# A fused involution block: another order for the norm chain, another engine for the constant part

## The chip, the cores and the metric

The kernel runs on one core of a Trainium2 chip. Its engines are PE (TensorE, matmuls; PEld is its weight load), DVE (VectorE), ACT (ScalarE), POOL (GpSimd) and SP (SyncE, which here only issues DMAs). Each engine takes its own instructions in order and waits on semaphores for the others. The metric is the device time of one execution in microseconds (us).

## The reference, cut to what matters

The input is x of 8 images, 256 channels, 56 x 56, in float32. Two layers follow each other:

```
x = x + involution(group_norm(x))            # this is where the change is
x = x + tri_conv_block(group_norm(x))        # two 3x3 convolutions, batch norms, ReLU
```

The involution makes, for each pixel, a 7 x 7 kernel for each of 16 groups of channels, and applies it to the pixel's neighbourhood:

```
ker = w_reduce @ v + b_reduce                # 64 channels, v = group_norm(x)
ker = w_span @ ker + b_span                  # 16 groups x 49 taps
out = (ker * patches(v)).sum(taps)           # zero padding of 3
```

Group norm is v = rstd * x + shift, with one rstd and one shift (-mean * rstd) per image and group. As it is linear, the sum over taps splits in two: rstd times the sum over the raw x, and shift times the sum of the kernel's 49 taps. The second is called the constant part here. It is itself a small matmul of the reduced `ker` with the taps' summed weights, plus the summed bias.

## The kernel before, in words

The involution is the first stage, to about 1031 us; two convolutions and a last elementwise stage follow, which the change does not touch.

The involution works by quarters: `quarters` (L1034) lists 8 images x 4 quarters c of 64 channels, and in a quarter both halves of the image's height lie side by side on 128 partitions. Each quarter has 10 rows `ty` of three image lines. r = c * 10 + ty numbers the rows of an image from 0 to 39. A row has, in the order of the text (L1055 to L1086):

- `apply_row` (PE, L905): the row's matmuls of neighbourhoods `q` with the kernels `a` into a PSUM tile `pa`, of which there are two. `prefetch` issues the load of a later `q` on SP's queue, and stores and loads of x are issued ahead of it.
- a step of the generator `norm`, if one is running.
- `gn2_stats` and `gn1_stats` (DVE, L153): bn_stats for the next layer's norm and for the next image's. The latter is spread over r = 4 to 19, one piece a row.
- `pick_out`: ACT scales the first part of `pa` into `inv` (L915), DVE adds the rest (L917), POOL adds `inv` to x (L922).
- `surround`: POOL adds the rim to a later `q` (L797); ACT fills its end (L810). `rim_of` prepares the rim in row 1.
- a second step of `norm`.
- `PER_ROW[ty]` steps of `gen`, the generator of the next quarter's kernels (`generate`).
- in rows 24 to 34 of an image, a strip of `reduce` for the next image (PE L759, ACT L768 into `kr`, with the bias `brn`).
- a step of `quant`, which quantizes the convolutions' weights on DVE (L314 to L334, tiles `piece_w`).

`pin` then fixes this order on every engine; no scheduler changes it.

`generate` has 14 units. A unit takes a pair of the six PSUM banks of `ps_p`, fills them by PE (L867, `pg`), and has one bank emptied by ACT with a bias (L871) and the other by DVE (L881). A pair is used again three units later, by a unit, by a strip or by the constant part. Units 0 to 5 read kr[0], units 6 to 9 kr[1], units 10 to 13 kr[2].

After its units, `generate` runs `constant` in two steps. Each has PE make the sums in a pair of banks (L832, `ks`), ACT turn them into `add` with the scale and the bias of the norm (L840), and POOL add `add` to x (L847); in the very last quarter DVE does that addition. Image lines of phase 0, 1, 2 have 504 columns each; the fourth piece is the last line of a half, with 56. In the steady loop both steps fall in row 8.

`params`, the norm chain of the next image, starts in r = 20 and is advanced twice a row, once ahead of the pick-out and once behind it. Its steps before the change:

- 20, ahead: matmul of the group means (L160), which needs the last bn_aggr.
- 20, behind: DVE's L164, L168, L169 (deviation `d`, squared).
- 21, ahead: matmul of `d` (L172).
- 21, behind: variance and `ve` (DVE L175, L139), the square root (ACT L141), the reciprocal and its Newton step (L143 to L149), scale and shift (L177, L178), and the image's scaled weights `wrn`, `scales`, `shift` (L670, L677, L680), all in one block.
- 23, ahead: matmuls of the reduce bias (L686); 23, behind: `brn` (L689).
- 24, ahead: rim matmuls (L696) and their copy by ACT (L700).

The small matmuls L160, L172 and L686 write to the spare columns of the current row's `pa`. In the last image, `gn2_params` takes the place of `params`: the same chain up to the norm's scale and shift, for the second layer. The first image's chain runs in the setup, as does the first quarter's `generate`.

Of the kernel before, what the change touches and what calls it, by code (L numbers as in the profile page):

```python
# [8 lines left out]
F32 = mybir.dt.float32  # L9
F32R = mybir.dt.float32r  # L10
AF = mybir.ActivationFunctionType
ALU = mybir.AluOpType
# [5 lines left out]
P = 128  # L18
B, C, H, W = 8, 256, 56, 56
# [5 lines left out]
GN_EPS = 1e-5  # L25
# [4 lines left out]
NCQ = C // CH  # L30
# [31 lines left out]

PER_ROW = (2, 2, 2, 1, 2, 2, 1, 2, 2, 0)
NQB = 5
# [3 lines left out]
NCB = 4  # L68
NC = NHW // NCB


# [20 lines left out]
def involution_tri_block_kernel(  # L92
# [41 lines left out]

    def rstd_of(var, eps, name):

        n = var.shape[1]
        ve = small.tile([P, n], F32, tag=f"rs_ve{n}", name=f"ve_{name}")
        nc.vector.tensor_scalar(ve, var, eps, None, ALU.add)  # L139
        sq = small.tile([P, n], F32, tag=f"rs_sq{n}", name=f"sq_{name}")  # L140
        nc.scalar.activation(sq, ve, AF.Sqrt)  # L141
        r0 = small.tile([P, n], F32, tag=f"rs_r0{n}", name=f"r0_{name}")
        nc.vector.reciprocal(r0, sq)  # L143
        e = small.tile([P, n], F32, tag=f"rs_e{n}", name=f"e_{name}")
        nc.vector.tensor_tensor(e, r0, ve, ALU.mult)
        nc.vector.tensor_tensor(e, e, r0, ALU.mult)
        nc.vector.tensor_scalar(e, e, -0.5, 1.5, ALU.mult, ALU.add)
        r = small.tile([P, n], F32, tag=f"rs_r{n}", name=f"r_{name}")
        nc.vector.tensor_tensor(r, r0, e, ALU.mult)  # L149
        return r  # L150

# [3 lines left out]
    def group_norm_params(mv, dst, psum_tile, name, means=None):  # L155
# [19 lines left out]
        nc.vector.tensor_tensor(var, ps2[:, :n], gm[:, :, 1], ALU.add)  # L175
        rs = rstd_of(var, GN_EPS, name)
        nc.vector.tensor_copy(dst[:, :, 0], rs)  # L177
        nc.vector.scalar_tensor_tensor(dst[:, :, 1], gm[:, :, 0], -1.0, rs, ALU.mult, ALU.mult)  # L178

# [440 lines left out]
    with ExitStack() as ph1:  # L620
# [6 lines left out]
        def ps_pair(name):  # L627
            return [ps_bank(f"{name}_{i}") for i in range(2)]
# [34 lines left out]
        def params(b, sums=None):  # L663
# [20 lines left out]
            for c in range(NCQ):  # L684
                for i in range(2):
                    nc.tensor.matmul(ps[i * CR:(i + 1) * CR, :1], wr[:CH, c, :], dst[:CH, c, 1:2],  # L686
                                     start=(c == 0), stop=(c == NCQ - 1))
            yield
            nc.vector.tensor_tensor(brn, br, ps[:, :1], ALU.add)  # L689
            yield  # L690
            if sums is not None:
# [127 lines left out]
        def constant(b, c):  # L819

            n = (TY - 1) * TX
            xv = xs[b, c][:, :(TY - 1) * PY * W].rearrange("p (t y w) -> p y t w", y=PY, w=W)
            scale, bias = prm[b][0][:, c, 1:2], prm[b][2][:, c:c + 1]
            for i0 in (0, 2):
                ps = ps_pair(f"ks_{b}_{c}_{i0}")
                add = work.tile([P, 2 * PX * n], F32, tag="add", name=f"add_{b}_{c}_{i0}")
                for i in range(2):
                    py = (i0 + i) % PY
                    k0, m = (0, n) if i0 + i < PY else (NT, TX)
                    rows = slice(i * CR, (i + 1) * CR)  # L830
                    for h in range(2):
                        nc.tensor.matmul(ps[i][h * CH:(h + 1) * CH, :PX * m], wsx[rows, c, :],  # L832
                                         kr[py][rows, :, k0 + h * m:k0 + (h + 1) * m],
                                         start=True, stop=True)
                for i in range(2):
                    py = i0 + i
                    m = n if py < PY else TX
                    v = add[:, i * PX * n:i * PX * n + PX * m].rearrange(
                        "p (t w) -> p t w", w=W)
                    nc.scalar.activation(  # L840
                        v.rearrange("p t (k x) -> p t k x", x=PX),
                        ps[i][:, :PX * m].rearrange("p (x t k) -> p t k x", x=PX, k=TX),
                        AF.Identity, bias=bias, scale=scale)
                    x_ = xv[:, py] if py < PY else xs[b, c][:, PY * (TY - 1) * W:].rearrange(
                        "p (t w) -> p t w", w=W)
                    engine = nc.vector if (b, c) == (B - 1, NCQ - 1) else nc.gpsimd
                    engine.tensor_tensor(x_, x_, v, ALU.add)  # L847
                yield

        def generate(b, c, a, shared=()):  # L850

            whole, rest = (v.rearrange("q t (g p) -> q g p t", g=GQ) for v in views(a))
            for u, (gp, p0, n) in enumerate(UNITS):
                ps = ps_pair(f"pg_{b}_{c}_{u}")
# [28 lines left out]
                yield  # L885
            yield from constant(b, c)

# [21 lines left out]
        def pick_out(b, c, ty, ps, n, m):  # L909
# [95 lines left out]
        first = params(0, sums)  # L1005
        for _ in range(8):
            next(first)
        nc.scalar.dma_start(wl, w_line)
# [39 lines left out]
        for m, (b, c) in enumerate(quarters):  # L1048
# [6 lines left out]
            for ty in range(TY):  # L1055
# [196 lines left out]
```

## Time and profile before

| | us |
|---|---|
| median of 3 runs (lowest, highest) | 2143.46 (2142.48, 2144.44) |
| the profiled execution | 2144.3 |
| its span, first to last instruction | 2142.5 |
| busy in the span: PE, DVE, ACT, POOL | 1750.4, 1760.6, 1428.7, 584.1 |
| first row of the loop, start | 56 |
| last row of the loop, start | 1031 |

A line of a group of instructions reads: source line, engine, operation, output<-inputs with their shape, count | busy time in us, mean ns of one | idle time of the engine just before them, and what ended it. A line of waits reads: who waited <- for whom: total us, times, longest. In a timeline the first two numbers are start and length in us, and the bracket at the end is the idle time before it and what ended that. "issue" is a time for which the profile shows nothing waited for. Line numbers are those of the kernel before.

### The profile page before, as it was taken

To read this page: it belongs to the slowest core of one execution; us is meant where nothing else is said; L and a number is where in the kernel's file an instruction comes from. 1 tells how busy PE (TensorE), PEld (TensorE's weight loads), DVE (VectorE), ACT (ScalarE), POOL (GpSimd) and SP (SyncE) were. 2 spreads that over 40 slices of the span, in tenths; PEclk is the share of its full clock that TensorE was granted. 3 is DMA by queue.
4 is the path that set the end of the run, shared out by engine and by line. 5 is a ranking of instruction groups with operands and counts; after the bars stand their busy time and mean duration, and the time that the engine had idled before them with its cause. 6 is when DMAs were issued, how large, how long until landed. Compare 5 with 4: busy or idle time off the path is not lost.

```text
span 2142.5 us, 70728 instructions
## 1 busy us (share of the span) xinstructions
PE 1750.4 (82%) x29680; PEld 1621.5 (76%) x29680; DVE 1760.6 (82%) x3360; ACT 1428.7 (67%) x3537; POOL 584.1 (27%) x960
## 2 busy tenths in 40 slices
PE   5898898989898897988799999998999999960000
PEld 5787777868777686877799999998999999950000
DVE  6778879787777878777899999998999999984444
ACT  4877787877778687777466666665676666653343
POOL 1655566555655555565000000000000000000000
PEclk9999999999999899999899999999999999985555
DMA  5767677686757768677633333335333333369999
GB/s 186 235 181 235 208 237 237 198 254 199 254 180 245 223 179 254 180 205 210 235 123 123 123 123 123 123 123 203 112 139 125 120 126 123 122 270 428 430 429 393
DMA packets 155370, 440.06 MB, mean 205 GB/s; under 512 B 63006, under 2 KB 73116, under 8 KB 147628
## 3 DMA queue, kind: packets, MB, share of 16 engines
q1 hardware_dynamic: 149760, 403.89, 55.2%
q10 hardware_dynamic: 5004, 31.56, 3.5%
q8 instruction: 235, 3.85, 0.7%
q14 instruction: 83, 0.68, 0.1%
q0 software_dynamic: 288, 0.08, 0.0%
HBM read 323.28 MB, written 112.20 MB: 203 GB/s over the span
## 4 chain that ended last, share of the span: by engine, by line
PE 69%; DVE 11%; DMA 9%; issue 5%; ACT 4%; POOL 1%; SPq 0%; ACTq 0%; POOLq 0%; DVEq 0%
PE c L561 39%; PE pg L867 15%; PE pa L905 9%; PE pk L759 4%; DMA y1f<-y1d 3%; DMA x1f<-x1d 2%; ACT a L871 2%; PE ks L832 2%; DMA out_y<-x1f 2%; DMA y2f<-y2d 1%; DVE inv L917 1%; DVE x1f L1164 1%; DVE a L881 1%; DVE st L153 1%; ACT add L840 1%
## 5 line engine op out<-in xcount | busy, mean ns | idle before, releaser
L561 PE MATMUL c<-pl,wq 128*128 128x392 f32 x4608 | 858.0, 349 | 11.3 <-ACT pl L433 9.2
L561 PEld LDWEIGHTS c<-pl,wq 128*128 128x128 f32 x4608 | 855.1, 190 | 13.9 <-ACT pl L433 9.6
L871 ACT ACTIVATE a<-pg,bt 126x126 f32<-126x126 f32 x2028 | 524.8, 457 | 110.8 <-PE pg L867 110.5
L867 PE MATMUL pg<-kr,wl 64*126 64x140 f32 (+1 forms) x6144 | 456.3, 291 | 43.2 <-ACT a L871 17.3
L867 PEld LDWEIGHTS pg<-kr,wl 64*126 64x126 f32 x6144 | 395.3, 194 | 72.7 <-issue 28.5
L905 PE MATMUL pa<-a,q 126*32 126x48 f32 x17024 | 289.0, 215 | 63.7 <-issue 55.6
L905 PEld LDWEIGHTS pa<-a,q 126*32 126x32 f32 x17024 | 241.1, 116 | 128.9 <-issue 86.8
L881 DVE TENSOR_TENSOR a<-pg,bt 126x504 f32<-126x504 f32 (+4 forms) x640 | 280.8, 481 | 37.4 <-PE pg L867 35.9
L922 POOL TENSOR_TENSOR x<-x,inv 128x168 f32<-128x168 f32 x310 | 161.1, 520 | 394.9 <-DVE inv L917 355.4
L917 DVE SCALAR_TENSOR_TENSOR inv<-pa,gn1s,inv 128x168 f32<-128x168 f32 (+1 forms) x384 | 134.0, 351 | 156.3 <-ACT inv L915 153.4
L410 ACT CAST pl<-r 128x812 fp32r<-128x812 f32 x190 | 160.7, 868 | 130.8 <-DVE r L405 121.5
L386 POOL MEMSET xp<- 128x116 f32 x32 | 6.3, 196 | 828.4 <-DVE a L405 805.1
L797 POOL TENSOR_TENSOR q<-q,sides 126x256 f32<-126x256 f32 (+1 forms) x320 | 225.7, 706 | 7.8 <-DMA q<-in_x_nb 7.8
L411 DVE TENSOR_TENSOR pl<-r,pl 128x812 fp32r<-128x812 f32 x190 | 185.3, 1002 | 28.0 <-ACT pl L410 26.7
L491 ACT ACTIVATE dummy<-y,nc 128x1568 f32<-128x1568 f32 (+1 forms) x128 | 200.2, 1564 | 4.8 <-DVE y L581 3.5
L915 ACT ACTIVATE inv<-pa,gn1s 128x168 f32<-128x168 f32 x320 | 133.3, 417 | 62.8 <-PE pa L905 47.6
L153 DVE BATCH_NORM_STATS2 st<-x 128x6 f32<-128x392 f32 x256 | 138.0, 555 | 7.9 <-DMA x<-in_x 7.4
L847 POOL TENSOR_TENSOR x<-x,add 128x504 f32<-128x504 f32 x124 | 123.2, 1024 | 12.6 <-ACT add L840 12.6
L1131 ACT ACTIVATE xp<-raw,bi_bn,sc_bn 128x392 f32<-128x392 f32 (+1 forms) x125 | 83.0, 721 | 60.3 <-DVE a L405 58.9
L1111 ACT ACTIVATE xp<-raw,gn 128x392 f32<-128x392 f32 (+1 forms) x125 | 83.3, 721 | 52.7 <-DVE a L405 51.6
L1162 DVE SCALAR_TENSOR_TENSOR y1f<-y2f,sc_bn,y1f 128x3136 f32<-128x3136 f32 (+2 forms) x20 | 56.6, 2831 | 62.8 <-DMA y2f<-y2d 52.5
L759 PE MATMUL pk<-x,wrn 64*128 64x168 f32 (+1 forms) x1152 | 101.8, 317 | 0.1
(186 smaller groups left out, 1812.0 us busy)
## 6 DMA issues: line engine op xcount, KB each, us to landing
q<-in_x_nb SPq DMA_DIRECT2D x320, 448.0 KB, 4.2
raw<-x1d SPq DMA_DIRECT2D x32, 812.0 KB, 7.0
raw<-y1d SPq DMA_DIRECT2D x32, 812.0 KB, 5.9
x1d<-x SPq DMA_DIRECT2D x64, 392.0 KB, 5.2
x<-in_x SPq DMA_DIRECT2D x60, 392.0 KB, 5.2
y1d<-y SPq DMA_DIRECT2D x30, 784.0 KB, 3.3
y2d<-y SPq DMA_DIRECT2D x30, 784.0 KB, 3.8
y1f<-y1d SPq DMA_DIRECT2D x14, 1568.0 KB, 15.1
```

The lines of the kernel that those rows point to most:

```text
L153: nc.vector.bn_stats(st[:, j, :], xt[:, j * NC:(j + 1) * NC])
L410: nc.scalar.copy(hi, r)
L411: nc.vector.tensor_tensor(lo, r, hi.bitcast(F32), ALU.subtract)
L491: nc.scalar.activation(dst, v, f, bias=shift[:, to:to + 1], accum_out=stats[:, to, j, n:n + 1])
L561: nc.tensor.matmul(ps[:, to, :NM], wq[k][:, t, dx, to * P:(to + 1) * P], part[:, t, :, dx:dx + W], start=(c == 0), stop=(c == last))
L759: nc.tensor.matmul(ps[h][:, :m * W], wrn[rows, c, :], src[rows, r0:r0 + (m - 1) * PY + 1:PY, :], start=(c == 0), stop=(c == NCQ - 1))
L797: nc.gpsimd.tensor_tensor(v, v, z, ALU.add)
L867: nc.tensor.matmul(dst, wl[rows, c, gp, o:o + NQ], kr[py][rows, px, :], start=True, stop=True)
L871: nc.scalar.activation(dst[:, g + 1, p0 + j], ps[1][:NQ, j * nt + t0:j * nt + t1], AF.Identity, bias=bt[:, c, g + 1, p0 + j:p0 + j + 1])
L881: nc.vector.tensor_tensor(dst[:, g, p0:p0 + n].rearrange("q p t -> q t p"), ps[0][:NQ, t0 * n:t1 * n].rearrange("q (t p) -> q t p", p=n), ...
L905: nc.tensor.matmul(ps[o:o + m, k * w:(k + 1) * w], q[:NQ, k, o:o + m], av[:, t + k, g * w:(g + 1) * w], start=True, stop=True)
L922: engine.tensor_tensor(xv, xv, iv.rearrange("p t (y x) -> p y t x", x=PX), ALU.add)
```

## The change

Three things are done.

The constant part leaves ACT and POOL. DVE reads the sums from PSUM, multiplies by the norm's shift and adds x in one instruction, in place. The norm's bias, which does not depend on the pixel, goes into the pick-out's activation. The pieces are paired anew: phase 0 and the last line (both from kr[0]) come in one step right after unit 5, phases 1 and 2 (kr[1], kr[2]) in the last step. With the new `PER_ROW` the steps fall in row 3 and row 8, rows 4 to 7 have two units each, and row 3 has none. In quarter 2, row 3 (r = 23) comes ahead of the strips of rows 24 to 27 that write kr[0].

The norm chain gets two steps more: the generator stops ahead of the square root and behind it. `ve` is made in 21 behind, the square root in 22 ahead, and the block from the reciprocal on in 22 behind. The reduce bias's matmuls and `brn` share a step, 24 ahead; the rim comes in 25 behind.

The statistics of the next image end in r = 18, which has two pieces, and no longer in 19.

```diff
-PER_ROW = (2, 2, 2, 1, 2, 2, 1, 2, 2, 0)
+PER_ROW = (2, 2, 2, 1, 2, 2, 2, 2, 1, 0)
+CONST_AT = 5
...
+STATS_AT = {r: (r - 4,) for r in range(4, 18)} | {18: (14, 15)}
...
-    def rstd_of(var, eps, name):
+    def rstd_of(var, eps, name, rs):
...
         sq = small.tile([P, n], F32, tag=f"rs_sq{n}", name=f"sq_{name}")
+        yield
         nc.scalar.activation(sq, ve, AF.Sqrt)
+        yield
         r0 = small.tile([P, n], F32, tag=f"rs_r0{n}", name=f"r0_{name}")
...
-        return r
+        rs.append(r)
...
-        rs = rstd_of(var, GN_EPS, name)
-        nc.vector.tensor_copy(dst[:, :, 0], rs)
-        nc.vector.scalar_tensor_tensor(dst[:, :, 1], gm[:, :, 0], -1.0, rs, ALU.mult, ALU.mult)
+        rs = []
+        yield from rstd_of(var, GN_EPS, name, rs)
+        nc.vector.tensor_copy(dst[:, :, 0], rs[0])
+        nc.vector.scalar_tensor_tensor(dst[:, :, 1], gm[:, :, 0], -1.0, rs[0], ALU.mult, ALU.mult)
...
-            yield
             nc.vector.tensor_tensor(brn, br, ps[:, :1], ALU.add)
-            yield
+            yield "bias"
+            for _ in range(2):
+                yield
...
-            scale, bias = prm[b][0][:, c, 1:2], prm[b][2][:, c:c + 1]
-            for i0 in (0, 2):
-                ps = ps_pair(f"ks_{b}_{c}_{i0}")
-                add = work.tile([P, 2 * PX * n], F32, tag="add", name=f"add_{b}_{c}_{i0}")
-                for i in range(2):
-                    py = (i0 + i) % PY
-                    k0, m = (0, n) if i0 + i < PY else (NT, TX)
+            for pair in ((0, PY), (1, 2)):
+                ps = ps_pair(f"ks_{b}_{c}_{pair[0]}")
+                for i, py in enumerate(pair):
+                    k0, m = (0, n) if py < PY else (NT, TX)
...
-                    nc.scalar.activation(
-                        v.rearrange("p t (k x) -> p t k x", x=PX),
-                        ps[i][:, :PX * m].rearrange("p (x t k) -> p t k x", x=PX, k=TX),
-                        AF.Identity, bias=bias, scale=scale)
...
-                    engine = nc.vector if (b, c) == (B - 1, NCQ - 1) else nc.gpsimd
-                    engine.tensor_tensor(x_, x_, v, ALU.add)
+                    x_ = x_.rearrange("p t (k x) -> p t k x", x=PX)
+                    nc.vector.scalar_tensor_tensor(
+                        x_, ps[i][:, :PX * m].rearrange("p (x t k) -> p t k x", x=PX, k=TX),
+                        prm[b][0][:, c, 1:2], x_, ALU.mult, ALU.add)
                 yield
...
+            made = constant(b, c)
             for u, (gp, p0, n) in enumerate(UNITS):
...
                 yield
-            yield from constant(b, c)
+                if u == CONST_AT:
+                    next(made)
+                    yield
+            yield from made
...
-            nc.scalar.activation(iv, parts[:, :, 0], AF.Copy, scale=scale[:, 0:1])
+            nc.scalar.activation(iv, parts[:, :, 0], AF.Identity, bias=prm[b][2][:, c:c + 1],
+                                 scale=scale[:, 0:1])
...
-                if more and 4 <= r < 20:
-                    gn1_stats(b + 1, (r - 4) // NCB, (r - 4) % NCB)
+                for k in STATS_AT.get(r, ()) if more else ():
+                    gn1_stats(b + 1, k // NCB, k % NCB)
```

More of the change, by code (lines that the diff above doesn't have):

```diff
@@ L832, in constant @@
                         nc.tensor.matmul(ps[i][h * CH:(h + 1) * CH, :PX * m], wsx[rows, c, :],
-                                         kr[py][rows, :, k0 + h * m:k0 + (h + 1) * m],
+                                         kr[py % PY][rows, :, k0 + h * m:k0 + (h + 1) * m],
                                          start=True, stop=True)
-                for i in range(2):
-                    py = i0 + i
+                for i, py in enumerate(pair):
                     m = n if py < PY else TX
-                    v = add[:, i * PX * n:i * PX * n + PX * m].rearrange(
-                        "p (t w) -> p t w", w=W)
-                    nc.scalar.activation(
-                        v.rearrange("p t (k x) -> p t k x", x=PX),
-                        ps[i][:, :PX * m].rearrange("p (x t k) -> p t k x", x=PX, k=TX),
-                        AF.Identity, bias=bias, scale=scale)
                     x_ = xv[:, py] if py < PY else xs[b, c][:, PY * (TY - 1) * W:].rearrange(
                         "p (t w) -> p t w", w=W)
-                    engine = nc.vector if (b, c) == (B - 1, NCQ - 1) else nc.gpsimd
-                    engine.tensor_tensor(x_, x_, v, ALU.add)
+                    x_ = x_.rearrange("p t (k x) -> p t k x", x=PX)
+                    nc.vector.scalar_tensor_tensor(
+                        x_, ps[i][:, :PX * m].rearrange("p (x t k) -> p t k x", x=PX, k=TX),
+                        prm[b][0][:, c, 1:2], x_, ALU.mult, ALU.add)
                 yield
@@ L1005, in involution_tri_block_kernel @@
         first = params(0, sums)
-        for _ in range(8):
-            next(first)
+        while next(first) != "bias":
+            pass
         nc.scalar.dma_start(wl, w_line)
```

## The prediction

> **What bounds the kernel now.** I looked first at the page's busy line and slices. No engine is the bound of the whole: PE and DVE both stand at 82% of the span, and the slices show three stages, the involution (to about 1031 us), two convolutions and a tail. Every edit is in the involution, so I read that stage alone.
>
> ```profile
> PE 1750.4 (82%) x29680; PEld 1621.5 (76%) x29680; DVE 1760.6 (82%) x3360; ACT 1428.7 (67%) x3537; POOL 584.1 (27%) x960
> ```
>
> The second view was busy time by stretch, in us, for the four quarters of one image, 0 to 3 in order, and for the stretch behind its norm chain. Columns: stretch, length, busy time of PE, PEld, DVE, ACT, POOL, then the granted PE clock and DMA.
>
> ```profile
> 669.60:698.39 28.79, 23.79 (x750) 19.56 (x748) 24.05 (x66) 22.55 (x82) 19.30 (x31) 1.00 0.88 294
> 698.39:728.21 29.82, 24.71 (x751) 20.83 (x748) 28.23 (x78) 22.12 (x80) 17.12 (x28) 0.94 0.76 234
> 728.21:768.00 39.79, 35.94 (x864) 31.25 (x862) 28.33 (x86) 27.58 (x96) 21.99 (x34) 0.87 0.54 159
> 768.00:797.10 29.10, 27.64 (x810) 23.90 (x808) 21.06 (x58) 23.90 (x88) 14.20 (x25) 1.00 0.71 201
> 738.90:749.10 10.20, 9.58 (x162) 8.29 (x162) 7.02 (x32) 5.42 (x24) 3.37 (x7) 0.50 0.45 121
> ```
>
> So the last quarter is PE's (95%). Quarter 1 is DVE's (95%). Quarter 2, with the norm chain, is 10 us longer than its neighbours, and 10.2 us of it run at half the PE clock. The third view was the waits of PE from 56 to 1031 us (total, times, longest).
>
> ```profile
> PE pa L905 <- issue: 55.6, 51, 3.9
> PE pg L867 <- ACT a L871: 17.1, 16, 2.4
> PE pg L867 <- DVE a L881: 10.8, 8, 2.2
> PE pa L905 <- POOL q L797: 4.8, 6, 1.6
> PE pa L172 <- DVE d_a L169: 4.5, 4, 1.2
> PE pa L160 <- DVE mv L661: 3.9, 3, 1.5
> ```
>
> "issue" falls in the middle of runs of like matmuls; the change has as many matmuls, so I leave it. The timeline then says what lies behind the other rows. First, the end of a quarter:
>
> ```profile
> 698.41 4.07 POOL L847 TENSOR_TENSOR x<-x,add 128x504 f32<-128x504 f32 x4
> 698.64 1.13 DVE L322 TENSOR_SCALAR piece_w<-piece_w 128x48 f32<-128x48 f32 x1
> 701.09 1.20 DVE L330 SCALAR_TENSOR_TENSOR piece_w<-piece_w 128x48 f32<-128x48 f32 x1
> 705.09 1.86 PE L867 MATMUL pg<-kr,wl 64*126 64x140 f32 x12 [1.99 <-DVE a L881]
> ```
>
> L322 and L330 take 0.19 and 0.20 us when undisturbed; under POOL's L847 they take 1.1 to 1.2. DVE falls behind, its L881 comes late, and PE waits 1.99. Second, the norm chain, rows 20 to 22:
>
> ```profile
> 732.08 1.17 DVE L169 TENSOR_TENSOR d_a<-d_a 128x4 f32<-128x4 f32 x1
> 733.30 0.39 PE L172 MATMUL pa<-d_a,grp_sb 128*128 128x4 f32 x2 [1.06 <-DVE d_a L169]
> 737.99 0.20 ACT L141 ACTIVATE sq_a<-ve_a 128x4 f32<-128x4 f32 x1 [3.80 <-DVE ve_a L139]
> 739.09 0.83 PE L867 MATMUL pg<-kr,wl 64*126 64x140 f32 x2 [2.37 <-ACT a L871]
> ```
>
> ACT stands 3.80 us at the square root with row 21's L871 behind it; those hold the PSUM banks, so PE waits 2.37, and then runs at half clock.
>
> [...] L330 is blocked, the L881 of 504 elements, one input from PSUM, stays at 0.68. [...]
>
> **Part one, the constant part (32 quarters).**
> Removed from ACT: L840, 96 of 771 ns and 32 of 405 ns, 67.2 + 13.0 = 80.2 us. Removed from POOL: L847, 115.1 + 9.4 = 124.5 us. Removed from DVE: 4 of L847 in the last quarter, 2.7 us.
> Added to DVE: 96 long and 32 short scalar_tensor_tensor from PSUM. Long ones at the 678 ns of L881's 504-element form (same source, same size): 65.1. Short ones at the 272 ns of L917's 56-element form: 8.7. Sum 73.8. [...] The strided read is not seen on DVE; if it costs as much as DVE's own blocked L847 (867 ns) the sum grows by 18.
> Given back to DVE: the piece_w operations cost some 83 us more than at their minimum (for L331, (512 - 195) ns x 64 = 20; the other eight likewise). POOL's L847 has 22% of POOL's time, so at least 18; matched by overlap about 34. I take 26. DVE net: 73.8 - 2.7 - 26 = +45 us, 1.4 a quarter.
> Added to ACT: pick-out's L915 gets a bias pointer. [...] In rows where DVE waits for L915 (120.3 us in all) [...] PE has slack there: I take 3 us lost, 0 to 9.
> What PE may get back: waits for L881, 10.8; for POOL's q, 4.8; for DVE's inv, 2.5; and half-clock stretches of 3.4 us at 182.5, 452, 705 and 834, half of 13.6 = 6.8. Together 24.9. Not all: quarters 0 and 1 have DVE at 84 to 95%, and 1.4 us more a quarter leaves part of the stall, now for DVE's own work. I take 18, from -15 (16 DVE-bound quarters x 0.9) to 25. The setup's constant part, ahead of row 0, loses 4 L840 and 4 us of POOL: +2.
> The unit moved from row 3 to row 6 makes rows 4 to 7 four full ones. [...] ACT falls back about 1.5 us; three bank pairs cover about that, and rows 8 and 9, now without L840, let it catch up. Cost nothing; if the cover is gone, 1.4 us x 31 = 43.
>
> **Part two, the norm chain (7 images and the last one's gn2 form).**
> The cost now: waits at L160 3.9, at L172 4.5 + 1.0, at L867 behind ACT 17.1, 26.5 in all. Half clock in rows 20 to 26: 51.0 us over the images, of which PE is busy 48.9; half of it is lost, 24.5. Sum 51.
> L160: the statistics end in row 18 and not 19, so this wait goes. One bn_stats (0.56) only changes rows.
> L172: it keeps its place; d and d*d lose the blocking (L169 0.27 instead of 1.17), but DVE brings 1.26 us of constant part from row 18. 0.7 a time stays: 5.6.
> Square root: `ve` is made in row 21 and read in row 22, so ACT's 3.8 goes, and 17.1 with it.
> The rest of the chain is a block on DVE, about 3.7 us in the timeline (reciprocal to gn1b), now in row 22 ahead of that row's four L881. PE finds cover in row 23 (pa 0.73, ks 0.7) and in pa and br of row 24 (0.73 + 0.8); the L881s end some 1.5 us later. So PE's next unit in row 24 waits 1.5, and the strip, whose banks the constant part's two DVE reads hold, 0.5. Another new wait: brn now stands ahead of row 24's pick-out, so ACT's L915 waits for DVE there, with row 24's L871 behind it; it ends about when DVE's L881 do. 2.0 x 7 = 14. The br matmuls and the rim only change rows. No DMA is added or moved.
> Half clock left: I take 10 of 24.5. Left in all: 5.6 + 14 + 10 = 29.6. Gain 51 - 29.6 = 21.4, from 0 to 51.
>
> **Sum.** 21.4 + 18 + 2 - 3 = 38.4. The profiled execution took 2144.3 us, span 2142.5 and 1.8 around it; 2144.3 - 38.4 = 2105.9. It lies 0.8 above the median of the runs, so 2105.
>
> **Rivals.**
> A, the forecast: both parts pay in part. 2105, own range 2090 to 2122. Chance 0.55.
> B, all relieved: both stalls go, as the PE-bound last quarter suggests, and DVE's block is hidden. 51 + 25 gives 2068; I allow 2066 to 2090. Against it: DVE at 95% in quarter 1. Chance 0.16.
> C, the wait moves: DVE's added 45 us eat the gain of part one, and the block in row 22 with the wait on brn eats most of part two. Gain 10, 2133, range 2122 to 2148. For it: DVE's shares. Chance 0.19.
> D, slower: DVE becomes the bound. If its 45 us come on the path in full and the read from PSUM takes the 867 ns (+18), part two's 21 and the setup's 2 do not pay: 2143.5 + 63 - 23 = 2183 at the worst; 2160 as a middle. [...] Chance 0.10.
>
> Measurement tells 0.2%, 4.3 us, from no change. Faster: A, B and 0.14 of C, 0.85; same 0.05; slower 0.10. The range leaves out the lower part of B and D with the end of C: 2074 to 2141.
>
> **What would show it.** PE's waits for the square root's row (L867 behind ACT) go from 17.1 to under 5, and the wait before the mv matmul is gone. piece_w operations drop by 18 to 34 us in sum. The new DVE operation takes about 0.68 us. DVE's share in quarter 1 stays above 93%. Quarter 2 goes from 38 to 35 us, quarters 0 and 1 from 29 to 28. After the chain's block a wait for DVE appears at row 24. I am wrong if quarters 0 and 1 grow, which is D, if rows 6 and 7 show PE waiting for L871, or if PE's stalls return as "issue", which would hold the gain down.

## The result

| | before | after |
|---|---|---|
| median of the runs of the comparison, us | 2144.44 | 2132.84 |
| profiled execution, us (its span) | 2144.3 (2142.5) | 2127.57 (2125.8) |
| loop, first to last row, us | 975.0 | 959.9 |

The ratio of after to before is 0.9937, with a 95% interval from 0.9923 to 0.9952. The change gains 0.63%, some 13.5 us, where 38.4 were forecast. Medians differ from chip to chip (before alone had medians from 2141 to 2153 over the comparisons below), so every experiment is read by its ratio to the runs of before on its own chip. 0.1% is 2.1 us. Where two kernels are compared through before, their ratios are divided; the interval of such a quotient is about 0.3% either side, and that the ratio of after to before is the same on each of the chips is taken for granted. Line numbers in a run's view are those of its own kernel.

Busy time of the engines of after:

```profile
PE 1737.7 (82%) x29680; PEld 1606.0 (76%) x29680; DVE 1778.4 (84%) x3484; ACT 1376.1 (65%) x3409; POOL 462.3 (22%) x836
```

ACT has lost 53 us, of the 80.2 that the forecast took from it with L840, and POOL 122, for the forecast's 124.5. DVE has gained 18 and not 45. Then the same quarters of the same image as before the change, and the stretch behind its norm chain (row 24). Columns: stretch, length, busy time of PE, PEld, DVE, ACT, POOL, granted PE clock, DMA share and GB/s.

```profile
664.49:695.81 31.32, 27.33 (x740) 22.41 (x741) 25.42 (x69) 20.59 (x76) 15.24 (x27) 0.84 0.86 265
695.81:728.28 32.47, 25.75 (x744) 21.85 (x741) 28.80 (x85) 21.54 (x77) 13.17 (x25) 0.89 0.74 227
728.28:764.52 36.24, 33.06 (x848) 28.54 (x849) 28.69 (x90) 24.30 (x88) 15.40 (x27) 0.95 0.57 167
764.52:794.10 29.58, 27.39 (x807) 23.54 (x806) 21.24 (x61) 23.70 (x86) 13.07 (x24) 1.00 0.66 197
738.81:747.36 8.55, 6.35 (x123) 5.80 (x121) 8.17 (x31) 2.86 (x10) 3.36 (x6) 0.80 0.53 161
```

In this image quarter 2 is 3.6 us shorter, but quarters 0 and 1 are each over 2.5 us longer, at a lower granted clock (0.84 for 1.00, 0.89 for 0.94). Over images 1 to 6 the mean lengths of quarters 0 to 3 went from 29.32, 29.17, 38.28 and 28.33 us to 30.75, 29.13, 35.67 and 28.14. So quarter 2 gained 2.6 an image, near the 3 that were forecast, and quarter 0 gave 1.4 of it back. The latter need not be the change's doing: in e1 below, whose quarter 0 has the instructions of before, its mean is 30.99 us, so single executions differ by as much. The waits of PE in after's loop (total, times, longest):

```profile
PE pa L908 <- issue: 66.0, 60, 4.1
PE pg L867 <- issue: 16.8, 12, 2.7
PE pa L177 <- DVE d_a L174: 6.0, 6, 1.9
PE pg L867 <- DVE a L881: 3.9, 8, 1.0
PE pk L766 <- DVE x L844: 3.3, 4, 1.1
...
PE pg L867 <- ACT a L871: 0.5, 1, 0.5
```

L867 behind ACT went from 17.1 to 0.5 and L867 behind DVE from 10.8 to 3.9. The wait ahead of the first norm matmul (L160 before, L165 now) is gone, and the one for POOL's q fell from 4.8 to 0.3. The wait at the second norm matmul (L177, L172 before) stayed: 7.8 with its smaller lines, 5.5 before. And "issue" has grown from 69.5 to 82.8 us. The timeline of after's norm chain, for the same image:

```profile
735.96 0.20 ACT L145 ACTIVATE sq_a<-ve_a 128x4 f32<-128x4 f32 x1 [0.40 <-DVE ve_a L142]
736.40 0.74 PE L867 MATMUL pg<-kr,wl 64*126 64x140 f32 x6 [0.81 <-DVE a L881]
...
740.46 0.45 PE L692 MATMUL pa<-gn,wr 64*64 64x1 f32 x9 [0.84 <-DVE gn L184]
...
742.27 0.39 PE L692 MATMUL pa<-gn,wr 64*64 64x1 f32 x7 [1.36 <-issue]
```

The square root holds ACT for 0.40 us where it held it for 3.80. What is late next is DVE's block, ahead of row 24's bias matmul. The end of quarter 0 in the timeline of after shows DVE's L328 and L336 (L322 and L330 before) undisturbed:

```profile
697.01 0.19 DVE L328 TENSOR_SCALAR piece_w<-piece_w 128x48 f32<-128x48 f32 x1
698.50 0.20 DVE L336 SCALAR_TENSOR_TENSOR piece_w<-piece_w 128x48 f32<-128x48 f32 x1
```

**An account of the loop.** I summed, from the records of PE's matmuls between the first and the last row, the idle time that ends in "issue", all other idle time, and the time at a lowered clock, of which half is taken as lost (the granted clock was 0.50 in each of these stretches of before and after). What is left over is between 799 and 816 us in every kernel of this study, most near 805, so these three terms carry most of the difference from kernel to kernel. One profile is one execution, though; the verdicts rest on the ratios.

| us in the loop | length | "issue" | other waits | lowered clock |
|---|---|---|---|---|
| before | 975.0 | 70.5 | 47.4 | 90.7 |
| after | 959.9 | 84.8 | 31.1 | 74.6 |
| e1, norm chain alone | 977.6 | 78.9 | 46.5 | 90.6 |
| e2, constant part alone | 970.5 | 89.4 | 29.3 | 93.7 |
| e7, POOL's work put back | 979.5 | 68.8 | 50.8 | 111.2 |
| e9, half of the q loads, short lead | 977.1 | 53.2 | 60.4 | 102.0 |
| e12, DVE relieved by ACT | 981.1 | 100.8 | 29.6 | 97.1 |
| e15, half of the q loads, full lead | 946.0 | 74.0 | 24.1 | 85.7 |
| e18, x loads early | 966.4 | 89.2 | 26.3 | 94.6 |

From before to after the other waits fell by 16.3 and "issue" rose by 14.3. PE is idle as long as before (117.9 and 115.9). Of the 15.1 us by which this loop of after is shorter, 8 are half of the lowered clock, 2 are idle time, and 5 are in the rest.

### The profile page after: what moved, and what is told of

The parts are those of the page before. It is cut to its first block, busy times and chain, and to the rows that moved or that the text cites. A ratio compares the mean times of both kernels' runs of the same rounds, so it can differ in the third digit from the quotient of the medians.

```text
span 2125.8 us, 70519 instructions
## 1 busy us (share of the span) xinstructions
PE 1737.7 (82%) x29680; PEld 1606.0 (76%) x29680; DVE 1778.4 (84%) x3484; ACT 1376.1 (65%) x3409; POOL 462.3 (22%) x836
## 4 chain that ended last, share of the span: by engine, by line
PE 69%; DVE 12%; DMA 10%; issue 5%; ACT 4%; POOL 0%; SPq 0%; ACTq 0%; DVEq 0%; POOLq 0%
PE c L567 40%; PE pg L867 14%; PE pa L908 8%; PE pk L766 4%; DMA x1f<-x1d 4%; DMA y1f<-y1d 2%; ACT a L871 2%; PE ks L836 2%; DVE a L881 2%; DVE inv L921 1%; DVE x1f L1168 1%; DVE x L844 1%; DMA out_y<-x1f 1%; DVE st L158 1%; DMA y2f<-y2d 1%
## 5 line engine op out<-in xcount | busy, mean ns | idle before, releaser
L871 ACT ACTIVATE a<-pg,bt 126x126 f32<-126x126 f32 x2028 | 516.6, 457 | 82.2 <-PE pg L867 79.7
L867 PE MATMUL pg<-kr,wl 64*126 64x140 f32 (+1 forms) x6144 | 441.4, 290 | 24.2 <-issue 16.8
L867 PEld LDWEIGHTS pg<-kr,wl 64*126 64x126 f32 x6144 | 391.5, 194 | 46.0 <-issue 19.9
L908 PEld LDWEIGHTS pa<-a,q 126*32 126x32 f32 x17024 | 236.5, 114 | 158.4 <-issue 100.4
L918 ACT ACTIVATE inv<-pa,gn1b,gn1s 128x168 f32<-128x168 f32 x320 | 162.5, 508 | 160.8 <-PE pa L908 104.4
L766 PEld LDWEIGHTS pk<-x,wrn 64*128 64x128 f32 x1152 | 91.8, 192 | 16.8 <-issue 9.6
## 6 DMA issues: line engine op xcount, KB each, us to landing
y1f<-y1d SPq DMA_DIRECT2D x14, 1568.0 KB, 15.1
```

The source lines that it names most:

```text
L766: nc.tensor.matmul(ps[h][:, :m * W], wrn[rows, c, :], src[rows, r0:r0 + (m - 1) * PY + 1:PY, :], start=(c == 0), stop=(c == NCQ - 1))
L867: nc.tensor.matmul(dst, wl[rows, c, gp, o:o + NQ], kr[py][rows, px, :], start=True, stop=True)
L871: nc.scalar.activation(dst[:, g + 1, p0 + j], ps[1][:NQ, j * nt + t0:j * nt + t1], AF.Identity, bias=bt[:, c, g + 1, p0 + j:p0 + j + 1])
L908: nc.tensor.matmul(ps[o:o + m, k * w:(k + 1) * w], q[:NQ, k, o:o + m], av[:, t + k, g * w:(g + 1) * w], start=True, stop=True)
L918: nc.scalar.activation(iv, parts[:, :, 0], AF.Identity, bias=prm[b][2][:, c:c + 1], scale=scale[:, 0:1])
```

## The experiments

Theory F: PE's supply of instructions is the next limit; what is freed of other waits comes back as "issue". Theory D: DVE is the next limit; its added work eats the gain.

### The parts alone: e1 to e4

e1 is before with the norm chain's edits alone:

```diff
+STATS_AT = {r: (r - 4,) for r in range(4, 18)} | {18: (14, 15)}
...
+        yield
         nc.scalar.activation(sq, ve, AF.Sqrt)
+        yield
...
-            yield
             nc.vector.tensor_tensor(brn, br, ps[:, :1], ALU.add)
-            yield
+            yield "bias"
+            for _ in range(2):
+                yield
```

> The kernel before with the norm chain's edits alone (two more steps, brn in the step of its matmuls, statistics to row 18); the constant part stays on ACT and POOL in row 8. Theory F (PE's instruction supply takes up what the removed waits free): the profile of the change shows quarter 2 shorter by 2.6 us an image and quarters 0, 1 and 3 the same in sum, so this part gives 10 to 18 us, all that the change gives. Theory D (DVE's added constant part eats a larger gain of the chain): this part alone gives 20 us or more, and the constant part loses 8 or more. The prediction had 21 for it.

e2 is before with the constant part's edits alone (its rows and its pick-out's bias as in after; the chain as in before):

```diff
-                    engine.tensor_tensor(x_, x_, v, ALU.add)
+                    nc.vector.scalar_tensor_tensor(
+                        x_, ps[i][:, :PX * m].rearrange("p (x t k) -> p t k x", x=PX, k=TX),
+                        prm[b][0][:, c, 1:2], x_, ALU.mult, ALU.add)
```

> The kernel before with the constant part's edits alone (DVE from PSUM, rows 3 and 8, bias in the pick-out); norm chain and statistics as before. Theory F: within 6 us of the kernel before, as the waits for L881 and for POOL go, but the wait behind the square root stays and issue grows. Theory D: slower by 5 us or more. The prediction had 17 faster for it.

e3 is after with both steps of the constant part in row 8 again, and e4 is before with the steps in rows 3 and 8, but still made by ACT and POOL. "Exclusion" in the expectations of e4 and e7 stands for what before's trace shows: DVE's L330 takes 0.20 us undisturbed, and up to 1.24 beside POOL's L847.

```diff
-PER_ROW = (2, 2, 2, 1, 2, 2, 2, 2, 1, 0)
-CONST_AT = 5
+PER_ROW = (2, 2, 2, 1, 2, 2, 1, 2, 2, 0)
+CONST_AT = -1
```

> The changed kernel with both steps of the constant part in row 8 and the units per row of before. If the place in the rows matters (DVE gets 2.3 us in one row, with PE's next unit behind it), slower than the change by 5 to 15 us. If only the engine matters, within 4 us of the change.

And e4's:

```diff
-            for i0 in (0, 2):
+            for i0, pair in ((0, (0, PY)), (2, (1, 2))):
...
-            yield from constant(b, c)
+                if u == CONST_AT:
+                    next(made)
+                    yield
+            yield from made
```

> The kernel before with the constant part split over rows 3 and 8 as in the change, but still done by ACT and POOL. POOL's L847 then comes in two blocks of about 1.5 and 2.5 us. If the row alone matters, faster than before by 5 us or more; if the exclusion between DVE and POOL matters, about the time before (within 5 us), with piece_w operations as slow as before.

Measured, ratio to before: e1 0.9959 (0.9938 to 0.998), e2 0.9966 (0.9951 to 0.9982), e3 0.9955 (0.9931 to 0.9979), e4 0.9985 (0.9969 to 1.0001). So the chain alone is worth some 9 us, the constant part alone some 7, and they add up: 0.9959 x 0.9966 = 0.9925. For e1, Theory F had 10 to 18 us and Theory D 20 or more; for e2, F had at most 6 us either way and D a loss, so e2 speaks against D. Where the constant part's steps stand is worth at most a few us either way: e3 can't be told from after, and e4's interval reaches no change.

The place has another effect than time. In before, and in e1 and e3, the constant part of quarter 3 is made in row 28, behind the strips of rows 24 to 27 that overwrite kr[0] for the next image (in before's image 2 L768 writes the new kr[0] from 378.04 us on, and the sums of L832 start at 388.49). So in seven of the eight images phase 0 and the last line of that quarter take the next image's reduced kernels. The change, which makes them in row 23, takes the right ones.

The waits of PE in e1's loop:

```profile
PE pg L873 <- DVE a L887: 20.4, 16, 2.2
PE pa L176 <- DVE d_a L173: 11.7, 6, 2.8
```

The waits for ACT (17.1) and for the statistics (3.9) are gone, but those for DVE's `a` went from 10.8 to 20.4 and those at the second norm matmul from 5.5 to 12.3 with the last image's. In sum its waits other than "issue" are 46.5 for 47.4: the wait moved. The waits of PE in e2's loop (up to 1020 us; the loop ends at 1026):

```profile
PE pa L902 <- issue: 67.5, 61, 3.8
PE pg L861 <- issue: 16.8, 13, 2.6
PE pa L161 <- DVE mv L662: 10.0, 7, 2.1
```

Here the waits other than "issue" fell by 18.1 us, from 47.4 to 29.3. "issue" rose by 18.9, from 70.5 to 89.4. The 18.1 are a balance: the waits for DVE's `a` went from 10.8 to 1.4, those for ACT from 17.1 to 8.2 at L867 (L861 here), and the wait for the statistics rose from 3.9 to 10.0.

### DVE, more and less: e7, e8, e12

e7 puts work of L847's size back on POOL: behind each of DVE's new reads, POOL squares a scratch tile. e8 has DVE do each new read twice, the second time into scratch.

```diff
+                    z = spare[:, :m * PX]
+                    nc.gpsimd.tensor_tensor(z, z, z, ALU.mult)
```

> The changed kernel with, behind each of the new DVE reads, an addition of one POOL instruction of the size of the removed L847 on a scratch tile that nobody waits for. If the exclusion between POOL and DVE is what the removal of L847 paid for, piece_w operations get 18 to 34 us slower in sum and the time rises by 4 to 10 us. If it paid for nothing (theory F takes all), within 3 us of the change.

```diff
+                    nc.vector.scalar_tensor_tensor(
+                        z, ps[i][:, :PX * m].rearrange("p (x t k) -> p t k x", x=PX, k=TX),
+                        prm[b][0][:, c, 1:2], z, ALU.mult, ALU.add)
```

> The changed kernel with each of the new DVE reads done twice, the second time into a scratch tile: 74 us more of DVE, no other engine waits for its result, but the PSUM banks come free later. Theory D: DVE is the bound in quarters 0 and 1, so the time rises by half of it or more, 30 to 70 us. Theory F: by less than 20 us, most of it hidden under issue.

e7 came to 1.0025 (1.001 to 1.004), e8 to 1.0092 (1.0061 to 1.0124). Against after that is 0.9% or 19 us for e7, where 4 to 10 were expected. Its nine piece_w operations take 218 us, for 182 in after, DVE is busy 35 us more, and PE waits for DVE where it did so little in after; its waits for POOL's q are 1.7 us:

```profile
PE pa L913 <- DVE piece_w L336: 14.2, 8, 2.4
PE pg L872 <- DVE a L886: 11.4, 19, 1.4
```

So freeing DVE from POOL is worth as much as the whole change gains. For e8 it is 1.6% or 33 us, some 0.45 us for each us of the 74 that DVE was given. Both are more than Theory F had (at most 3 and under 20), and e8 is within D's 30 to 70. So DVE has little room left: neither a full bound, at 1 for 1, nor free.

e12 takes work from DVE: units 5 and 13 have both banks emptied by ACT.

```diff
+BY_ACT = (5, 13)
...
+                for j in range(n if u in BY_ACT and not shared else 0):
+                    for dst, t0, t1 in parts:
+                        nc.scalar.activation(
+                            dst[:, g, p0 + j], ps[0][:NQ, t0 * n + j:t1 * n:n],
+                            AF.Identity, bias=bt[:, c, g, p0 + j:p0 + j + 1])
-                for dst, t0, t1 in parts:
+                for dst, t0, t1 in parts if u not in BY_ACT or shared else ():
```

> After with the a maps of units 5 and 13 taken out of PSUM by ACT alone, where after shares them between ACT and DVE: DVE has some 37 us less to do, ACT some 65 us more. D: the time falls by 0.3 to 0.45 of DVE's relief, 10 to 16 us, near 2120. F: the freed time comes back as issue, 0 to -4 us. If ACT is then late with these maps: PE waits for ACT in rows of those units, and the time is the same or up to 10 us more.

It came to 0.9964 (0.9947 to 0.998), no better than after. DVE's busy time fell by 25 us (1753.6) and PE's waits for ACT stayed under 2 us, but ACT was busy 56 us more, and DVE waited for it longer. The wait of DVE in after and in e12:

```profile
DVE inv L921 <- ACT inv L918: 118.5, 114, 3.9
DVE inv L927 <- ACT inv L924: 153.0, 126, 3.5
```

So D's 10 to 16 us did not come, but DVE did not get its room for nothing either, and the test leaves D open. "issue" rose from 84.8 to 100.8 while other waits fell by only 1.5, so the rise is not time that was freed of them.

### The load of DMA: e5, e6, e9, e10, e15, e16, e17

Instructions come by DMA too: the trace has queues of the kind "instruction". One of them in after's loop (packets, MB, share of the DMA engines):

```profile
q8 instruction: 195, 3.19, 1.4%
```

That is a packet of 16 KB every 4.9 us. By the trace's records of packets, of PE's stops for "issue" of over 0.8 us (37 in before, 39 in after) half end within 1.43 us after such a packet has landed, and nine in ten between 1.25 and 1.67 us after it. So I take this queue to be PE's. If the loads of q and x delay these packets, fewer loads must shorten the stops. The first pair, e5 from after and e6 from before, leaves out every second q load and reuses the tile of the row before:

```diff
-                loads[k] = load_q(*k)
+                loads[k] = load_q(*k) if k[2] % 2 == 0 else latest[0]
+                latest[:] = [loads[k]]
```

> The changed kernel with every second load of q left out: odd rows use the q tile of the row before, so the involution's sums are other numbers, with the same matmuls, the same rim additions and half of q's DMA. Theory F: the waits called issue come from PE's instructions arriving late behind other DMA packets, so they fall from 85 us to under 35 in the profile, and the time falls by 40 us or more against the change. Theory D (DVE is the bound): issue may fall, but the time falls by less than 15 us.

> The kernel before with every second load of q left out in the same way. Theory F: with instructions on time, the removed waits count in full, so this stays behind the changed kernel with half of q by 20 to 35 us, more than the 12 us of the full kernels. Theory D: the distance stays at about 12 us or shrinks.

0.9887 (0.9847 to 0.9926) and 1.0021 (1.0007 to 1.0035). This pair settles nothing: the odd row's rim addition had to wait for the even row's matmuls on the shared tile, and PE waited 55.0 and 44.7 us for it. The next pair, e9 and e10, sends the odd rows' additions and end copies to a scratch tile:

```diff
-NQB = 5
+NQB = 4
...
-            q = loads[b, c, ty][:NQ]
+            q = filled_in(b, c, ty)[:NQ]
...
-                nc.scalar.copy(loads[b, c, ty][:n, :, CH:],
+                nc.scalar.copy(filled_in(b, c, ty)[:n, :, CH:],
```

> After with half of the q loads left out: an odd row's matmuls read the q tile of the row before it as it stands, and that row's POOL additions at the rim and ACT end copies go to a scratch tile, so that no row waits for another row's matmuls. The sums are of other numbers than the reference's; every matmul, addition and copy is there. F (PE's instruction packets share the DMA queues' capacity with the loads, and the wait called issue takes up what is freed): issue falls from 85 us in the loop to 45 or less, with nothing in its place, and the time by 30 us or more, below 2105. D (DVE's added work is what holds the loop): issue falls, DVE's waits take its place, less than 15 us, 2118 to 2133.

> The same half of the q loads left out of before. The waits for ACT and for the norm chain (47 us in the loop) stay. F: issue falls from 70 to about 45, the time by 15 to 30 us, below 2129. D (in before DVE has 45 us less to do, so PE's own waits weigh more): as much or more than it gains in after. If the load of DMA has nothing to do with the loop's length, both stay within 5 us.

0.9951 (0.993 to 0.9972), the same as after within the interval, and 1.0045 (1.0026 to 1.0063). F's gain did not come. "issue" fell to 53.2 us and other waits rose by as much, as D had it, though for POOL. The timeline of e9 at the start of a row 20 shows by which way:

```profile
363.41 0.54 POOL L935 TENSOR_TENSOR x<-x,inv 128x168 f32<-128x168 f32 x1 [1.89 <-DVE inv L930]
363.90 0.46 POOL L813 TENSOR_TENSOR q<-q,tops 126x128 f32<-126x128 f32 x1
364.32 0.45 POOL L813 TENSOR_TENSOR q<-q,sides 126x128 f32<-126x128 f32 x1
364.41 0.69 PE L917 MATMUL pa<-a,q 126*32 126x48 f32 x8 [1.44 <-POOL q L813]
```

POOL stands 1.89 us waiting for DVE's `inv`, its addition to a later q is queued behind, and PE waits for that. But with four tiles I had also cut the lead from five rows to four, so that POOL's additions came two rows ahead of use and not three. e15 restores the lead and changes nothing else, e17 is the same for before, and e16 is e15 with e12's relief of DVE:

```diff
-        for _ in range(NQB):
+        for _ in range(5):
             prefetch()
```

> As the kernel with old q tiles, made from after, half of the q loads left out, but with five rows loaded ahead as in after, so that POOL adds the rim three rows ahead of use as in after. Of other numbers than the reference. F: the waits for POOL's q go below 5 us, issue stays below 55 us in the loop, and the time is 20 to 30 us below after, near 2107. D: the time stays within 8 us of after, and waits for what DVE writes (d_a, a, piece_w, inv, x) grow by what issue loses.

> The kernel with old q tiles and the same lead, and besides the maps of units 5 and 13 emptied by ACT alone, which takes some 25 us of busy time from DVE. Of other numbers than the reference. Both limits in balance: what neither did alone (0 us each) now comes, 15 to 25 us below after, near 2112. F: as e15_old_q_same_lead. D alone: 8 to 11 us below after, as ACT's relief alone should have given and did not. ACT bound (it has 50 us more): no gain, and PE's waits for ACT grow over 15 us.

> Before with half of the q loads left out and the lead of five rows kept, the counterpart of e15_old_q_same_lead (which was 24 us below after). Of other numbers than the reference. F as the place where the gain went (the load of DMA holds after more than it holds before): 5 to 15 us below before, ratio above 0.993, so that the change itself would be worth about twice as much with light DMA. The load holds both alike: 20 to 28 us below before, ratio 0.987 to 0.991, and the gain is lost elsewhere.

e15: 0.9825 (0.9798 to 0.9852), 24 us below after, which is F's number. The waits of PE in e15's loop:

```profile
PE pa L917 <- issue: 53.9, 54, 3.7
PE pg L876 <- issue: 19.3, 15, 2.8
...
PE pa L917 <- POOL q L813: 0.4, 1, 0.4
```

The wait for q is gone, as F had it; "issue" is 74.0 in the account and not under 55, so F's size for the wait itself is wrong. Nor did the packets themselves get much faster: their median is 0.99 us in after and 0.98 in e15, and one in ten takes over 1.54 us in after, over 1.34 in e15. e16: 0.9845 (0.9818 to 0.9872), not better than e15; relieving DVE by way of ACT still gains nothing (DVE's wait for ACT's `inv` went from 103.3 to 149.3). e17: 0.9911 (0.9885 to 0.9937), 19 us below before. It lies between its two forecasts, and the change is worth 0.9% with light loads (0.9825 / 0.9911 = 0.9913) against 0.6% with full ones, which the intervals can't tell apart. So the loads hold both kernels by about 20 us; that they are where the change's gain went is not shown.

### The x loads in other rows: e18

In after, quarter 0 has six of the eight x loads of the next image, the highest DMA share (0.86) and the lost time. e18 issues four of the eight in quarters 2 and 3 of the image before, as soon as their buffers are free:

```diff
+        X_EARLY = {26: (0, 0), 28: (0, 1), 36: (1, 0), 37: (1, 1)}
...
-                elif more and r in X_AT:
+                elif r in X_EARLY and b + 2 < B:
+                    load_x(b + 2, *X_EARLY[r])
+                elif more and r in X_AT and (b == 0 or X_AT.index(r) > 3):
```

> After with the x loads of the next image's quarters 0 and 1 issued in rows 26, 28, 36 and 37 of the image before, when their buffers have just come free, instead of rows 0, 1, 4 and 5; loads and sums are the same. F with the DMA load of quarter 0 as its cause: quarter 0 goes from 30.75 to about 29.3 us, quarters 2 and 3 gain at most 0.3 each, so some -8 us against after, near 2125. If the load only moves the stalls: 0 us, quarter 2 or 3 longer by what quarter 0 loses. D: 0 us.

It came to 0.9882 (0.9856 to 0.9908): 0.55% or 12 us below after, 25 below before. Mean quarters are 29.50, 29.87, 35.77 and 28.54 us. Against after's profile quarter 0 lost 1.25 us as F said; quarter 1 gained 0.74, which no theory had, and the four sum to 123.7 us in both. The profiled execution was the slowest of e18's six, and its loop is longer than after's (966.4 for 959.9), so the gain rests on the runs alone, and where in the loop it comes from is not shown. This version computes the same sums as after, and its runs beat both kernels.

### The chain by a half row or a row: e11, e14, e19

After still waits 7.8 us at the second norm matmul. e11 has the first one right behind row 19's pick-out and the second at the head of row 21; e14 has only the second one half a row later, behind row 21's pick-out. The edits of both, e11's first:

```diff
-        PARAMS_AT = 20
+        PARAMS_AT = 19
...
-                    norm = params(b + 1) if more else gn2_params(0, b)
+                    norm = chain([None], params(b + 1) if more else gn2_params(0, b))
...
         nc.vector.tensor_tensor(d, d, d, ALU.mult)
         yield
+        yield
         ps2 = psum_tile(f"gnp2_{name}")
```

```diff
+        yield
         ps2 = psum_tile(f"gnp2_{name}")
...
-            for _ in range(3):
+            for _ in range(2):
                 yield
             ps = ps_one(f"br_{b}")
```

> After with the chain's first matmul straight behind row 19's pick-out, the mean and variance steps at 20 and the second matmul at 21, where after has all of it in one row; the same instructions. F: the 7.6 us of waits of the second matmul go to below 2 us, and issue takes most of it back: -4 to 0 us. D: DVE does the same work, 0. If the second matmul's wait is on the path that sets the end: -6 to -8 us, near 2126.

> After with the chain's second matmul half a row later (behind row 21's pick-out) and one of the three empty steps in front of the bias matmul taken out, so that the bias stays in row 24; the same instructions. If the 7.6 us that PE waits at the second matmul are on the path at full price (the wait that the kernel with the chain a row up put in, 25.5 us for 7.6, cost about 17 us): -5 to -8 us against after, near 2125. F: issue takes most of it, -3 to 0. If the factors come too late for the strips of row 24: waits of pk for wrn, and no gain.

e11 came to 1.0018 (0.9995 to 1.0041), 17 us over after; e14 to 0.9993 (0.9978 to 1.0008), 12 over after. No theory had that. A wait of PE in e14's loop:

```profile
PE pa L178 <- DVE inv L922: 27.9, 8, 4.0
```

The norm chain's matmul writes to spare columns of the row's own `pa`. Ahead of the pick-out that tile is free; behind it the matmul must wait until DVE has read the row's sums (`inv`), 3.5 us each time. Row 21 grew from 3.6 to 7.1 us (mean of images 1 to 6). In e11 the first matmul met the same, 25.5 us in all.

e19 takes the second matmul a whole row later, ahead of row 22's pick-out, on top of e18:

```diff
-        yield
+        for _ in range(3):
+            yield
         ps2 = psum_tile(f"gnp2_{name}")
...
-            for _ in range(3):
-                yield
+            yield
             ps = ps_one(f"br_{b}")
```

> The kernel with early x loads, and the chain's second matmul a whole row later, ahead of row 22's pick-out, with two of the three empty steps in front of the bias matmul taken out, so that the bias stays ahead of row 24's pick-out; the same instructions. If it was the place behind the pick-out that cost 12 us in e14_second_matmul_later: the waits for d_a go below 1 us, none for inv comes in their place, and the time is 0 to 6 us below e18_x_loads_early, ratio 0.985 to 0.988. If the lateness of the chain cost it: waits for gn before the bias matmul or for wrn at the strips of row 24 over 10 us, ratio 0.992 to 0.996.

0.9959 (0.9942 to 0.9977), 17 us over e18. The wait at the second matmul is gone and no wait for `inv` came. But the bias matmul now waits 12.4 us for `gn`, and row 24 takes 8.5 us where after has 6.6:

```profile
PE pa L692 <- DVE gn L185: 12.4, 6, 2.9
```

So both matter: the place in the row and the lateness of the chain.

## Why the prediction was wrong

The direction and the outer range held; the size did not, by nearly three times, and the measured time is above the forecast's own range of 2090 to 2122. It is the number of rival C (2133), for part one by luck: C had DVE's 45 us eat that gain, where DVE got 18 and e2 shows "issue" in the place of the waits. For part two C was right in kind, as the waits moved to DVE, but not at the place that it named.

**The step that failed** is the sentence '"issue" falls in the middle of runs of like matmuls; the change has as many matmuls, so I leave it'. The number of matmuls stayed, the time did not: 70.5 to 84.8 us in the account. For the constant part the forecast counted 18.1 us of waits (10.8, 4.8 and 2.5) that PE would get back. In e2 all waits but "issue" fell by 18.1 too, of which some are others than those counted, and "issue" took 18.9. The text named this as what would hold the gain down, but gave it no term in the sum.

**The lowered clock** was forecast to give 14.5 us in quarter 2 and 6.8 in the other quarters. In quarter 2 it fell from 51.2 to 10.2 us, worth 20.5, more than forecast. In quarter 0 it rose from 13.7 to 34.1, a loss of 10.2, with quarter 0's idle time at 35.3 us before and 38.1 after (27.8 and 36.1 of it "issue"). These are single executions: e1, with quarter 0 as in before, has 28.7 us of lowered clock there, so the loss can't be put down to the change. Of after's 14 stretches of lowered clock, eleven have a stop for "issue" of over 1 us, up to 4.1, within 1.6 us of their start; of before's 20, seven.

**Part two, 21.4.** What goes was right: L160's wait, 17.1 behind ACT, 3.80 at the square root. What comes back was too small alone: the 5.6 us at L172 were 12.3 in e1, and the waits for DVE's `a` rose by 9.6. In after, with POOL's L847 gone, they are 7.8 and 3.9. So the part is worth some 9 us in the runs. The forecast wait of ACT for `brn` in row 24 is there, 35.8 us over seven images in after, 5 each, where 2.0 were priced, but PE hardly felt it: its waits for ACT are 6.2 us in the whole loop, none of them in row 24.

**Part one, 18 + 2 - 3 = 17.** It is worth 7. DVE's own terms erred on the cautious side, as this group of after shows:

```profile
L844 DVE SCALAR_TENSOR_TENSOR x<-ks,gn,x 128x504 f32<-128x504 f32 x95 | 67.0, 733 | 2.5 <-PE ks L836 2.4
```

The long read takes 733 ns, between the 678 taken and the bound of 867. POOL does not slow it as it did L330: 93 of all 96 overlap with work of POOL and took 733 ns in the mean, three do not and took 740, and none took over 744. The nine piece_w operations of which the largest was L331 fell from 223 to 182 us, 41 for the 26 taken and above the bound of 34. DVE is busy 18 us more, not 45, and its share in quarter 1 is 89%, not over 93%. So rival D had its size wrong too. That DVE's load keeps the gain is not shown: e12 and e16, which relieved DVE, gained nothing, though at the price of longer waits for ACT, while e7 and e8 show that more work on DVE does cost. ACT's pick-out with a second pointer:

```profile
L918 ACT ACTIVATE inv<-pa,gn1b,gn1s 128x168 f32<-128x168 f32 x288 | 149.8, 520 | 134.8 <-PE pa L908 78.3 <-DVE brn L694 35.8 <-POOL q L804 7.5
```

With the bias pointer, and Identity in place of Copy, it went from 429 to 520 ns, 91 more. The forecast's loss of 3 us by it was an estimate of mine, as were the 1.5 us by which ACT was to fall back in rows 4 to 7; rows 6 and 7 did not show ACT late.

**What stays open.** Shown is that the two kinds of idle time take each other's place: less of other waits brought more "issue" (e2), less "issue" brought waits for DVE by way of POOL (e9), and more waits brought less "issue" (e7). Their sum is 114 to 131 us in each kernel of the account but e15 (98), one execution of each. That each wait elsewhere is time in which PE's supply of instructions catches up would fit most of this, but it is a guess of mine and not shown: no run changed the number of PE's instructions, and that queue has 194 packets in before's loop and 195 in after's. Why halving the loads gained 24 us while "issue" fell by only 11 is open as well: the loops of the two profiles differ by 14 us, and the account covers those (11 and 7 of waits, less 5 to 6 for the lowered clock), not the 24 of the runs. Of the ten that are missing, 7 can be chance of the executions: after's profiled one lay 5.3 us under its median, e15's 2.0 over.

## What to carry to other kernels

Give the idle time without a named cause a term of its own in the sum: in e2 18.1 us of other waits went, "issue" took 18.9, and the runs gained some 7. Look at the profile of a single part of the change before crediting both: here the chain alone moved its waits to DVE, and the constant part alone moved them to "issue". A small matmul that borrows columns of a tile in use is better placed ahead of that tile's reader: behind it PE waited 27.9 us in e14. And a load may be worth moving to a stretch with a lower DMA share even where no engine is seen to wait for it: in e18 that gained 12 us over after.

## What the runs showed of the hardware

- PE's stops for "issue" of over 0.8 us end some 1.4 us (mostly 1.25 to 1.67) after a 16 KB packet of the instruction queue has landed; before has 194 of them in the loop and after 195, and the longest stop was 3.9 us and 4.1.
- Of the stretches at a granted clock of 0.50, one of 3.4 us in after follows a gap of 1.34 us and another one of 1.64; in before the one of 10.2 us at 738.9 comes with a gap of 2.37. They last 3.4, 6.8 or 10.2 us, one of after 23.9.
- Work on POOL that reads SBUF, with 104 us of busy time and nobody who waits for its result, cost 19 us of the kernel's time (e7), with 36 us more in DVE's piece_w operations.
- Half of the q loads left out gained 19 to 24 us, although PE waited for a load in neither kernel (0.3 us for after's q, 4.8 for before's, both for POOL's addition).
